# First messages as one tile and then three, an earlier clearing of bins, ten supertiles on the first 128 rows: a change to the opening of a graph kernel

## The chip, the cores and the metric

The kernel runs on one core of a Trainium2 chip. The metric is device time in microseconds (us), taken as the median of several executions. The core has five engines that run side by side and wait for one another through semaphores: TensorE (PE, matrix products; its weight loads are shown as PEld), VectorE (DVE), ScalarE (ACT), GpSimd (POOL) and SyncE (SP, which here only issues DMA transfers). ACT and POOL issue some transfers too.

## The reference

A layer of a graph network over 12,500 nodes with 128 features and 400,000 edges with 20 attributes. The edges are sorted by `dst`.

```
h    = relu(layernorm(x))                       # 12500 x 128
hW   = h @ W_in2f.T
Wij  = smu(edge_attr @ W_f1.T + b_f1) @ W_f2.T + b_f2
Wij  = Wij * edge_weight[:, None]               # 400000 x 128
msg  = hW[dst] * Wij                            # gather: dst is sorted
agg  = segment_sum(msg, src, 12500)             # scatter: src is random
out  = x + smu(agg @ W_o1.T + b_o1) @ W_o2.T + b_o2
smu(x) = ((1+a)x + (1-a) x erf(mu (1-a) x)) / 2,  a = 0.01, mu = 2.5
```

`smu` is computed as a scaled GELU plus a linear part.

## The kernel before

**Tiles.** 128 edges are a tile, 4 tiles a group (`GRP`), 8 tiles a supertile (`SUP`), so two groups make a supertile. There are 3125 tiles. The 12,500 nodes are 98 bins of 128 rows (`NB`). The supertiles are cut into ten epochs (`PARTS`: 59, 59, 59, 59, 48, ...). Each epoch has an area in device memory with room for a fixed number of rows for each bin; three areas (`buf`) are used in turn and are cleared beforehand.

**One group's way.** The helpers below are called by hand, in a written order that is each engine's order (the tile pools run under a manual schedule). For group g:
- `load` (SP) fetches the edge attributes into one of four filter buffers `fbufs` (128 rows by 1024 columns: 20 attribute rows, a row of ones for the bias, and further rows of ones that meet zero weights); `targets` fetches `rbc`, the edges' `dst` less a base, spread over all partitions; `window` fetches rows of h into `hw`.
- `pick` (DVE) or `pick_part` (ACT, two instructions a group) turns `rbc` into a one-hot matrix `oh`. The first `FEW` tiles use no window: their `dst` all lie in the first 128 rows, whose three bfloat16 parts are in `h_first`. Supertile 0 is picked by `pick_group` (DVE) from `dst` values that PE spread with transposes (`spread_group`).
- `hide` (PE, L625, `pu`), `bend` (ACT, L633, GELU, `ge`), `smooth` (DVE, L641, `sm`), `weigh` (PE, L678, `pw`): the filter network.
- `gather` (PE; L657 three products with `h_first`, L659 one with a window; `ph`), `take` (ACT, L667, `hg`), `mix` (DVE, L688, `mt`): the message, features on partitions.
- `turn` (PE, L699, four transposes, `pt`), `send` (ACT, L712 and L715, edge weight, `ms`), `scatter` (POOL, L726): four indirect transfers a group, one for each tile, each of which writes 128 message rows to the places in `ix`.
- `bins` (DVE, L556), `count` (PE, L570 to L573), `read` (DVE, L600), `number` (DVE, L612) find those places: a running count of each bin's rows.

In the main loop, iteration p does `turn`, `send`, a `step`, `number`, `weigh`, `gather`, `take`, `mix` (of the next group), a `step`, `hide`, `bend`, `count`, `smooth` (of the group after it), `pick_part`, `bins`, `read`, and a `step`. From the second epoch on, pieces of work on the epoch before (`parts`, L771 and L787) lie between.

**Steps.** `step` is called three times a group. It first empties the list `opening` (one entry a call): the normalized rows of bins 1 to 3 (`heads`, six stages) and the first 512 tiles' bases and bins (`one`: `based`, `spread`, `lowered`, `turned`, `written`, `bounded`, `binned`). After that it spreads some 280 further steps over the rest of the first epoch: the same for six more chunks of 512 tiles (`head_of`; `spread` is L353, `based` L344 to L348, `binned` L320 to L323, `limits` L377 and L378), the statistics and the h rows of the other bins, which `window` reads. `clear` in `chores` writes zeros to the areas through SP.

**Before the loop.** Loads on SP and ACT, constants on DVE and POOL, then by hand: the first `dst` values (`dsf`), row statistics of bin 0, its normalized, turned and rectified rows, `product` with `w_in`, the three parts `h_first` (`first_part`, `other_parts`), all stages of group 0, and most of group 1. The ACT table for GELU is loaded at L881, behind the square root of the deviations of bins 1 to 3. `quiet_ends` runs on POOL behind five small DVE writes (L425): zeros, the clearing of the last bin (L187, `buf<-zero`), fills of filter buffers 2 and 3. The scatters wait for the landing of that clearing.

## Time and profile before

| what | value |
|---|---|
| median of 3 runs | 4059.88 us (4059.31, 4059.88, 4063.59) |
| profiled execution, its own time | 4063.85 us |
| profiled execution, span of the core | 4062.1 us |
| granted TensorE clock over the span | 0.968 of full speed |
| busy: PE, PEld, DVE, ACT, POOL | 86%, 55%, 82%, 73%, 75% |
| scatters on POOL | 3125, the first at 19.4 us, the last at 3991.2 us |
| bytes moved | 760 MB, 187 GB/s |

A row of a timeline gives the start, the duration, the engine, the line, the operation with its output and inputs, the shape and the number of instructions that were merged; the bracket at its end gives the engine's idle time before it and what ended it. A row by stretches gives the length of the stretch, the busy time and instruction count for each engine, the granted clock, the DMA share and GB/s. Before the first clock record (at 9.6 us) the clock is shown as 1.00.

### The profile page before, as it was taken

Reading aid. Unit: us, or ns where it says so; the run is one execution under the profiler, and the core shown is the slowest. Engines: PE = TensorE matmul, PEld = TensorE weight load, DVE = VectorE, ACT = ScalarE, POOL = GpSimd, SP = SyncE. Lnnn points to the kernel's source line nnn. Section 1 sums busy time; section 2 is a strip of 40 time slices with the busy share of each in tenths; the row PEclk is TensorE's granted clock in tenths of the full one; section 3 lists DMA queues with packets and bytes.
Section 4 is the critical chain, followed back from the end, with each engine's and each line's share of the span. In section 5 each row is a group of like instructions: output and inputs, shape, how many; then the busy total and the mean of one; then the engine's idle time right before and its main releaser. Section 6 shows DMA issues by size and latency. Waiting matters only on the chain.

```text
span 4062.1 us, 69847 instructions
## 1 busy us (share of the span) xinstructions
PE 3492.8 (86%) x18417; PEld 2246.9 (55%) x18420; DVE 3328.4 (82%) x7355; ACT 2962.7 (73%) x7256; POOL 3042.2 (75%) x3168
## 2 busy tenths in 40 slices
PE   7777777999988999989999979999899979989657
PEld 3334434555555555555555546666566646656547
DVE  8987776888887888878888878888799869988447
ACT  5779986888886888877888877787777767766001
POOL 6777777777777777777777777777777777777775
PEclk9999998999999999999999999999999989999889
DMA  6976666777756565546565646666566657565987
GB/s 193 240 187 182 190 167 197 210 204 204 208 162 180 174 175 173 173 141 181 174 177 172 176 144 181 182 180 189 154 193 195 183 156 203 170 202 170 274 240 226
DMA packets 510392, 759.72 MB, mean 187 GB/s; under 512 B 174949, under 2 KB 313462, under 8 KB 509856
## 3 DMA queue, kind: packets, MB, share of 16 engines
q1 hardware_dynamic: 402416, 535.77, 48.4%
q0 software_dynamic: 100112, 207.06, 15.3%
q10 hardware_dynamic: 7456, 12.35, 0.8%
q8 instruction: 146, 2.39, 0.3%
q14 instruction: 262, 2.15, 0.2%
HBM read 460.77 MB, written 294.11 MB: 186 GB/s over the span
## 4 chain that ended last, share of the span: by engine, by line
PE 41%; DVE 26%; DMA 13%; ACT 9%; issue 6%; POOL 4%; ACTq 0%; SPq 0%; DVEq 0%; POOLq 0%
PE pw L678 13%; DMA buf<-ms,ix 10%; PE pg L787 10%; DVE se L771 9%; PE pu L625 7%; PE pt L699 7%; DVE mt L688 5%; POOL buf L726 4%; DVE sl L600 3%; ACT ms L715 3%; ACT ge L633 2%; DVE sm L641 2%; PE ph L659 2%; DVE so L556 2%; DVE agg L800 2%
## 5 line engine op out<-in xcount | busy, mean ns | idle before, releaser
L726 POOL DMA_INDIRECT buf<-ms,ix x2944 | 2829.0, 961 | 916.0 <-issue 270.6
L787 PEld LDWEIGHTS pg<-se,rw 128*128 128x128 f32 x8232 | 1080.8, 194 | 343.3 <-issue 277.1
L787 PE MATMUL pg<-se,rw 128*128 128x128 f32 x8232 | 1175.7, 282 | 96.4 <-DVE se L771 75.1
L715 ACT ACTIVATE ms<-pt,w_sb 128x128 f32<-128x128 f32 x3125 | 882.2, 363 | 196.8 <-PE pt L699 176.0
L556 DVE SCALAR_TENSOR_TENSOR so<-irow_ps,hi_f,so 128x98 f16<-128x98 f32 x2936 | 929.7, 317 | 78.0
L678 PE MATMUL pw<-sm,w_f 128*128 128x512 f32 x1564 | 884.1, 648 | 47.9 <-DVE sm L641 46.9
L625 PE MATMUL pu<-f,w_f 128*128 128x512 f32 x1564 | 813.6, 602 | 0.0
L633 ACT ACTIVATE ge<-pu 128x512 f32<-128x512 f32 x782 | 468.0, 598 | 443.6 <-PE pu L625 439.4
L771 DVE TENSOR_TENSOR se<-irow_ps,rw 128x1536 f32<-128x1536 f32 (+2 forms) x356 | 602.3, 1692 | 229.5 <-DMA rw<-buf 228.3
L699 PE MATMUL pt<-ident,mt 128*128 128x128 f32 x2944 | 468.9, 282 | 362.7 <-DVE mt L688 361.1
L688 DVE SCALAR_TENSOR_TENSOR mt<-pw,b,hg 128x512 f32<-128x512 f32 x782 | 583.4, 746 | 173.3 <-ACT hg L667 149.8
L641 DVE SCALAR_TENSOR_TENSOR sm<-pu,ge 128x512 f32<-128x512 f32 x782 | 534.2, 683 | 188.2 <-ACT ge L633 182.4
L699 PEld LDWEIGHTS pt<-ident,mt 128*128 128x128 f32 x2944 | 327.6, 142 | 447.2 <-DVE mt L688 444.4
L524 ACT ACTIVATE oh<-oh,onesb 128x512 bf16<-128x512 bf16 x770 | 555.5, 721 | 25.2
L523 ACT ACTIVATE oh<-rbc,nrow 128x512 bf16<-128x512 bf16 x770 | 551.2, 716 | 1.2 <-DMA rbc<-rel_dram 1.2
L667 ACT ACTIVATE hg<-ph 128x512 f32<-128x512 f32 x782 | 472.1, 604 | 99.9 <-PE ph L659 30.3
L600 DVE TENSOR_REDUCE sl<-pc 128x4 f32<-128x392 f32 x782 | 434.5, 556 | 0.0
L678 PEld LDWEIGHTS pw<-sm,w_f 128*128 128x128 f32 x1564 | 236.5, 191 | 161.8 <-DVE sm L641 124.7
L659 PE MATMUL ph<-oh,hw 126*128 126x512 bf16 x770 | 298.2, 387 | 0.0
L625 PEld LDWEIGHTS pu<-f,w_f 128*128 128x128 f32 x1564 | 256.9, 196 | 67.2 <-issue 57.9
L570 PE MATMUL pc<-so,tri 128*128 128x392 f16 x736 | 243.7, 331 | 1.7 <-DVE agg L425 1.7
L572 PEld LDWEIGHTS <-rest_h 128*128 128x128 f16 x781 | 76.7, 98 | 263.6 <-issue 263.6
(192 smaller groups left out, 2002.1 us busy)
## 6 DMA issues: line engine op xcount, KB each, us to landing
rw<-buf SPq DMA_DIRECT2D x300, 774.0 KB
rbc<-rel_dram SPq DMA_DIRECT2D x389, 256.0 KB
buf<-zero SPq DMA_DIRECT2D x146, 387.0 KB
buf<-ms,ix POOLq DMA_INDIRECT x2944
rw<-buf SPq DMA_DIRECT2D x49, 645.0 KB
f<-in_f_t SPq DMA_DIRECT2D x390, 80.0 KB
hw<-h_dram SPq DMA_DIRECT2D x770, 31.5 KB
kept_rows<-ms ACTq DMA_DIRECT2D x45, 258.0 KB
```

Of the source, the lines that this page charges most:

```text
L524: nc.scalar.activation(oh, oh, AF.Relu, scale=-1.0, bias=onesb[:, 0:1])
L556: nc.vector.scalar_tensor_tensor(so[:, j], irow_ps[:, :NB], hi_f[:, t + j:t + j + 1], so[:, j - 1] if j else before, op0=ALU.is_equal, op1 ...
L600: nc.vector.tensor_reduce(sl[:, :n], pc[:, :n], op=ALU.max, axis=AX.X)
L625: nc.tensor.matmul(pu[:, :n], w_f1, loaded[g // PER][0][:, o:o + n], start=True, stop=True)
L641: nc.vector.scalar_tensor_tensor(sm[:, :n], units_of.pop(g)[:, :n], LIN, hidden[g][:, :n], op0=ALU.mult, op1=ALU.add)
L678: nc.tensor.matmul(pw[:, :n], w_f2, hidden.pop(g)[:, :n], start=True, stop=True)
L688: nc.vector.scalar_tensor_tensor(mt[:, :n], pws.pop(g)[:, :n], b2, rows_of.pop(g)[:, :n], op0=ALU.add, op1=ALU.mult)
L699: nc.tensor.transpose(pt[:, j, :], mt[:, j * P:(j + 1) * P], ident)
L715: nc.scalar.activation(ms[:, j, 0:P], pt[:, j], AF.Copy, scale=w_sb[:, t + j:t + j + 1])
L726: i = nc.gpsimd.indirect_dma_start(out=bufs[k][:, :], out_offset=bass.IndirectOffsetOnAxis(ap=ix[:, j:j + 1], axis=0), in_=ms[:, j, :], in ...
L771: nc.vector.tensor_tensor(se[:, a:a + n], own.unsqueeze(1).to_broadcast([P, n, P]), rows_in[c][:, a:a + n, P:P + 1].to_broadcast([P, n, P] ...
L787: nc.tensor.matmul(pgs[0][:, g, :], rows_in[c][:, o, 0:P], sel[c][:, o, :], start=(q == 0), stop=(q == Q[k] - 1))
```

## The change

All of it is in the opening, but for the K range of `hide` and the rate of `step`.
- Group 0 is cut into its first tile (128 columns) and the other three (384 columns); the first tile's transposes, send and scatter stand ahead of the rest, and each tile is turned, sent and scattered by itself.
- The zeros and the clearing of the last bin are the first things that POOL does behind the constants; `quiet_ends` and its five DVE touches are gone.
- Constants for counting are made while the first loads are under way; `irow_ps` and the scaling of `w_f2` move to ACT; eight products that nobody reads (`idle`) stand first on PE.
- The deviations of bins 1 to 3 and the GELU table load stand ahead of `product`; their reciprocals become the first entry of `opening`.
- `FEW` is ten supertiles, not six; all but supertile 0 are picked on ACT with `pneg` as bias, and `pick` on DVE is gone.
- Only 21 rows of `w_f1` and of a filter buffer are read by `hide`; one buffer is filled with ones, the ones row is copied to the three others by DMA.
- `opening` takes an entry on every second call, and the later steps are spread over seven groups fewer.

```diff
+    def early_constants():
+        nc.vector.memset(onesb, 1.0)
+        nc.vector.memset(ones_h, 1.0)
+        nc.vector.memset(none, 0.0)
         nc.vector.tensor_scalar(lift, ident, BIG, None, op0=ALU.mult)
         nc.vector.scalar_tensor_tensor(tri, irow, pcol, lift, op0=ALU.is_gt, op1=ALU.add)
-        nc.vector.memset(ones_h, 1.0)
         nc.vector.tensor_sub(rest_h, ones_h, tri)
-        nc.vector.memset(none, 0.0)
+        nc.vector.tensor_scalar(pneg, pcol, -1.0, None, op0=ALU.mult)
+        nc.vector.memset(ones1, 1.0)
+        nc.vector.memset(bad, 0.0)
...
-        FEW = 6 * SUP
+        FEW = 10 * SUP
...
-        nc.sync.dma_start(ds, dst_col[:, 0:FEW])
         nc.scalar.dma_start(x_sb[:, 0:1, :], bin_rows(x, 0, 1))
         nc.sync.dma_start(ss, src_col[:, 0:FEW])
+        nc.scalar.dma_start(x_sb[:, 1:HEAD, :], bin_rows(x, 1, HEAD - 1))
         nc.scalar.dma_start(w_in, w_in_t)
+        nc.sync.dma_start(ds, dst_col[:, 0:FEW])
         fill(0, nc.vector)
-        fill(1, nc.vector)
-        nc.vector.tensor_copy(irow_ps, irow)
-        nc.gpsimd.memset(w_f1, 0.0)
+        early_constants()
+        nc.sync.dma_start(fbufs[0][0:R, :], f_t[:, 0:SUP * P])
         nc.sync.dma_start(w_f1[0:R, :], w_f1_t)
...
         nc.scalar.activation(spare[:, 0:1], eps, AF.Sqrt)
+        nc.scalar.activation(irow_ps, irow, AF.Copy)
+        nc.gpsimd.memset(zero, 0.0)
+        clear(0, len(cleans) - 1, nc.gpsimd)
+        nc.gpsimd.dma_start(h_dram[NB * P:N + P, :], zero[:N + P - NB * P, 0:3 * D // 2].bitcast(BF))
+        nc.gpsimd.memset(x_sb[:, NB - 1, :], 0.0)
+
+        def more_loads():
+
+            for i in range(1, NF):
+                nc.sync.dma_start(fbufs[i][R:R + 1, :], fbufs[0][R:R + 1, :])
+            load(1)
+            one["fetched"]()
+            nc.sync.dma_start(w_sb[:, FEW:CH], w_col[:, FEW:CH])
...
-            if s < FEW // SUP:
-                if i == 0:
-                    pick(s)
-                return
...
-            nc.scalar.activation(oh, loaded[s][1][:, o:o + n], AF.Abs, bias=nrow)
+            nc.scalar.activation(oh, loaded[s][1][:, o:o + n], AF.Abs, bias=pneg if s < FEW // SUP else nrow)
             nc.scalar.activation(oh, oh, AF.Relu, scale=-1.0, bias=onesb[:, 0:1])
...
-            nc.tensor.matmul(pu[:, :n], w_f1, loaded[g // PER][0][:, o:o + n], start=True, stop=True)
+            nc.tensor.matmul(pu[:, :n], w_f1[:R + 1], loaded[g // PER][0][:R + 1, o:o + n], start=True, stop=True)
...
+        def idle(n):
+            for _ in range(n):
+                nc.tensor.matmul(pt[:, 0:P], onesb, onesb, start=True, stop=True)
...
+        def turn_tile(j):
+            nc.tensor.transpose(pt[:, j * P:(j + 1) * P], mt[:, j * P:(j + 1) * P], ident)
+
+        def send_tile(j, ix):
+            nc.scalar.activation(ms[:, j, 0:P], pt[:, j * P:(j + 1) * P], AF.Copy, scale=w_sb[:, j:j + 1])
+            scatter_tile(0, ms, ix, j)
+
+        one_cut, others = (0, P), (P, (GRP - 1) * P)
+        idle(8)
+        stats(edge, 0)
+        nc.scalar.activation(rstd[:, 0:1], mv[:, 0:1, 1], AF.Sqrt, bias=eps)
+        nc.vector.tensor_copy(dsf, ds)
+        nc.vector.tensor_copy(ssf, ss)
+        stats(edge, 1)
+        scaled_means(0, 1)
         normed()
+        nc.tensor.transpose(pw[:FEW, 0:P], dsf, ident)
+        spread_tiles(0, pb0, 0, 2)
         turned()
+        nc.scalar.activation(few, pw[:FEW, 0:P], AF.Copy)
+        nc.sync.dma_start(rel_dram[0, 0:FEW * P].rearrange("(t e) -> t e", e=P), few)
+        more_loads()
+        for b in range(2, HEAD):
+            stats(edge, b)
+        shorn()
+        nc.scalar.activation(rstd[:, 1:HEAD], mv[:, 1:HEAD, 1], AF.Sqrt, bias=eps)
+        nc.scalar.activation(spare[:, 1:2], eps, AF.Gelu)
+        rounded(hi_f[:, 0:FEW], ssf)
+        bins(0)
+        hide_cut(*one_cut)
+        product()
+        spread_tiles(0, pb0, 2, 2)
+        first_part()
+        bend_cut(*one_cut)
         pick_group(0, pb0)
+        nc.scalar.activation(w_f2, w_f2, AF.Copy, scale=GC)
         other_parts()
         count(0)
+        gather_cut(*one_cut)
+        smooth_cut(*one_cut)
+        take_cut(*one_cut)
+        weigh_cut(*one_cut)
+        hide_cut(*others)
         read(0)
         number(0)
+        ix0 = taken.pop(0)
+        few_places()
+        mix_cut(*one_cut)
+        nc.scalar.activation(ms[:, :, P], lo_b[:, 0:GRP], AF.Copy)
+        bend_cut(*others)
+        gather_cut(*others)
+        turn_tile(0)
+        send_tile(0, ix0)
+        smooth_cut(*others)
+        weigh_cut(*others)
+        take_cut(*others)
         targets(1)
         load(2)
         targets(2)
+        pb1 = bank("pb")
+        spread_tiles(1, pb1, 0, GRP)
+        mix_cut(*others)
+        bins(1)
+        for j in range(1, GRP):
+            turn_tile(j)
+            send_tile(j, ix0)
         hide(1)
+        count(1)
         bend(1)
         pick_group(1, pb1)
         smooth(1)
         read(1)
-        pick(1)
+        pick_part(PER)
         bins(2)
+        pick_part(PER + 1)
...
-        opening = [one["based"], heads[0], one["spread"], heads[1], one["lowered"], heads[2], one["turned"], heads[3],
-                   one["written"], heads[4], one["bounded"], heads[5], one["binned"], other_starts]
+        opening = [lambda: scaled_means(1, HEAD), one["based"], heads[0], one["spread"],
+                   heads[1], one["lowered"], heads[2], one["turned"], heads[3], one["written"], heads[4], one["bounded"],
+                   heads[5], one["binned"], other_starts, rows_in_thirds]
+        apart_by = 0
...
             if opening:
-                opening.pop(0)()
+                apart_by += 1
+                if apart_by % 2 == 0:
+                    opening.pop(0)()
                 return
             slot += 1
-            while taken_steps < COUNT and taken_steps * 3 * (eps_of[0][1] * PER - 15) < slot * COUNT:
+            while taken_steps < COUNT and taken_steps * 3 * (eps_of[0][1] * PER - 22) < slot * COUNT:
```

`hide_cut` to `mix_cut` are the helpers of one group with a range of columns; `scatter_tile` is the body of `scatter`'s loop; `rows_in_thirds` makes `prow` and `nrow` as before.

More of the change, by code (lines that the diff above doesn't have):

```diff
@@ L877, in gnn_kernel @@
-        nc.vector.tensor_scalar(w_o1, w_o1, LIN, None, op0=ALU.mult)
-        for b in range(1, HEAD):
-            stats(edge, b)
-        deviations(1, HEAD)
-        nc.scalar.activation(spare[:, 1:2], eps, AF.Gelu)
-        product()
-        counting_constants()
-        bins(0)
-        quiet_ends()
-        load(1)
-        first_part()
-        bend(0)
+        nc.scalar.activation(few, pw[:FEW, 0:P], AF.Copy)
+        nc.sync.dma_start(rel_dram[0, 0:FEW * P].rearrange("(t e) -> t e", e=P), few)
```

116 lines of the change are left out of this document (49 added, 67 removed).

## The prediction

> **What bounds the kernel now.** I read the costliest groups first, then POOL's scatter by stretches, then the timelines of the opening. The page shows one group that nothing overlaps on its engine:
>
> ```profile
> L726 POOL DMA_INDIRECT buf<-ms,ix x2944 | 2829.0, 961 | 916.0 <-issue 270.6
> ```
>
> These scatters and 181 more of the same line (`ix_kept`) are POOL's whole work. By stretches (us, POOL busy and count, clock, DMA share, GB/s):
>
> ```profile
> 0.00:100.00 100.00, 57.62 (x59) 0.92 0.67 194
> ...
> 800.00:900.00 100.00, 75.92 (x80) 1.00 0.71 202
> ...
> 3700.00:3800.00 100.00, 75.93 (x80) 0.88 0.65 190
> ```
>
> 79 to 80 scatters in each full 100 us, whatever PE, DVE and ACT do: POOL is the bound, 1.264 us a scatter (0.96 busy, 0.30 issue). 3124 such steps are 3949 us. The rest of the 4062.1 us span is the first scatter's start (19.4), 71 us behind the last one (3991.2), and 23 us in which POOL waited. So I keep one number, the **zero line**: start of scatter n minus 1.264 n. Only what raises it costs time; the other engines' work is free while messages lie ready ahead of POOL. POOL's timeline, where it rises (second column: duration; bracket: idle before):
>
> ```profile
> 13.03 0.77 POOL L187 DMA_DIRECT2D buf<-zero  x1
> ...
> 19.42 1.05 POOL L726 DMA_INDIRECT buf<-ms,ix  x1 [3.59 <-ACT ge L633]
> ...
> 25.42 0.96 POOL L726 DMA_INDIRECT buf<-ms,ix  x1 [1.10 <-ACT ms L715]
> ...
> 64.21 0.96 POOL L726 DMA_INDIRECT buf<-ms,ix  x1 [3.17 <-ACT ms L715]
> ...
> 81.24 0.96 POOL L726 DMA_INDIRECT buf<-ms,ix  x1 [1.83 <-ACT ms L715]
> ```
>
> They are scatters 0, 4, 32 and 44: zero line 19.42, 25.42-5.06=20.36, 64.21-40.45=23.76, 81.24-55.62=25.62. Single scatters of 1.2 to 1.4 us bring it to 29.5 by 700 us, and 12.9 us come later, 9 of them in four waits between 2450 and 2639 us. Scatter 0 did not wait for its message (first `ms` write ended 17.41): POOL's first semaphore event on this line is at 18.6, when the zeros issued at 13.03 had landed. Groups 8 and 11 are late because of PE:
>
> ```profile
> 52.56 0.66 PE L699 MATMUL pt<-ident,mt 128*128 128x128 f32 x4 [0.28 <-DVE mt L688]
> 56.12 1.12 PE L353 MATMUL pg<-base_f,ones 1*128 1x512 f32 x2 [2.90 <-DVE base_f L345]
> ```
>
> In PE's order L353 (head 1's `spread`) stands behind `turn`, and its input behind `smooth`, `pick`, `bins` and `read` on DVE. The clock then falls, and head 1's `binned` and `limits` (4 us of DVE) follow: turns 7 to 11 start at 52.56 and 79.01, 26.5 us for 20.2 us of POOL. The clock by stretches (PE busy, PEld, DVE, ACT, POOL, clock):
>
> ```profile
> 9.59:13.00 3.41, 1.45 (x8) 0.59 (x7) 2.90 (x17) 1.67 (x6) 1.55 (x2) 1.00 0.00 0
> 13.00:16.41 3.41, 2.49 (x5) 0.92 (x6) 1.84 (x4) 0.45 (x2) 2.83 (x6) 0.50 0.68 184
> 16.41:19.83 3.42, 2.96 (x8) 1.14 (x6) 1.72 (x6) 1.74 (x5) 0.41 (x1) 0.50 0.80 264
> ```
>
> It changes at ends of 3.41 us stretches: down after 1.45 us of matmul, still down after 2.49, up after 2.96.
>
> The durations of the sum are starts to starts in the timelines. A pass of 512 columns on PE: 0.853 cold (L625 at 16.80 and 17.65), 0.427 warm (21.74 and 22.17); fp32 products take two passes, transposes one, and results come 0.2 behind. ACT in a late group, with picks:
>
> ```profile
> 66.05 0.60 ACT L633 ACTIVATE ge<-pu 128x512 f32<-128x512 f32 x1
> 66.53 0.73 ACT L523 ACTIVATE oh<-rbc,nrow 128x512 bf16<-128x512 bf16 x1
> 67.29 0.72 ACT L524 ACTIVATE oh<-oh,onesb 128x512 bf16<-128x512 bf16 x1
> 67.92 0.19 ACT L712 ACTIVATE ms<-lo_b 128x4 f32<-128x4 bf16 x1
> 68.02 1.12 ACT L715 ACTIVATE ms<-pt,w_sb 128x128 f32<-128x128 f32 x4
> ```
>
> `bend` 0.5, two pick instructions 1.4, and only then the sends: a pick on ACT delays its group's messages by 1.4 us, where the DVE pick that it replaces (0.48 for two groups) stood beside them.
>
> **First message.** DVE loses the second fill (0.91) and gains constants (`lift` 0.22, `tri` 0.35, `rest_h` 0.23, memsets about 0.3): `down` ends near 5.0, as before (5.08). Eight `idle` products of two 0.213 passes hold PE from 2.1 to 5.5; behind them three transposes end at 6.1, so `turned` runs as before and xT is ready at 6.9. `product` no longer stands behind a 512-column `hide` (6.40 to 8.39) but behind 128 columns (0.43). The deviations of bins 1 to 3 need DVE's statistics, now done near 6.0, not 8.2; so the table load (1.28) runs 7.2 to 8.5 and `first_part` starts 8.65, not 9.97. DVE then runs the residual 0.28, `pick_group` 0.74, third part 0.29, `smooth` 0.25, `read` 0.56, `number` 0.16, `few_places` 0.21, `mix` 0.27: 11.4. PE is later: 3 x 0.107 gather to 10.2, weigh 0.43 to 10.75, the other 384 columns of `hide` 2 x 0.64 to 12.0 and of `gather` 3 x 0.32 to 13.0, and `turn_tile(0)`, behind them in its order, to 13.4. `send` 0.37 and POOL's 0.28: first scatter 14.1; 14.6 if the first needs the 0.8 us seen between 18.6 and 19.42. The zeros are issued near 2.3 and land, at 5.5 us as before, by 8, under cover of 6 us. Uncovered bound: they share the DMA engines with the first loads and could delay those 1 to 2 us; `w_f2` and `w_sb` have 3 us.
>
> **Second message, second group.** Tile 1 waits for bend 0.48, smooth 0.53, weigh 2 x 0.64, mix 0.57, turn, send: 16.8 cold, 15.8 warm. The turns share one `pt` bank and alternate with sends, 0.85 a tile, so `hide(1)` starts at 17.4 cold or 16.4 warm (before: 16.80) and its `bend` at 19.3 or 17.5 (before: 18.75). Here the moved picks count: behind `bend(1)` ACT has four pick instructions (2.8), `take` 0.5, `bend(2)` 0.5, two picks 1.4, `ms` 0.1, send 0.37, and POOL 0.28: scatter 4 comes 6.5 behind `bend(1)` (before 6.67, on DVE's picks and a half-cold PE). Zero line at scatter 4: 19.0 if warm throughout, 20.9 if cold only until 19.8, 23.2 if cold until `hide(2)`. From 9.59 to 13.0 PE would have 2.98 us of matmul, so it rises at 13.0; the next stretch has about 1.5, next to the 1.45 that fell. I take 20.0. So five us at scatter 0 become 0.4 at scatter 4.
>
> [...]
>
> **Groups 2 to 13.** `heads[0]` puts 1.2 us of normalizing on ACT ahead of `send(2)`: +0.3. Then ACT needs 3.6 us a group with picks (65.08 to 69.24 with a 0.5 extra), PE 3.9; before, with opening steps at full rate, turns 1 to 7 took 4.75 each. At half rate I take 4.35, 0.7 below POOL's 5.06: by group 13 some 8 us lie ahead. Head 1's `based` and `spread` fall on the third and first step of groups 12 and 13, the same bad order, now against 8 us of cover, with 6.3 us of stall. So the rise from 20.72 to 25.62 goes, but for its 0.3 of slow scatters: -4.6. Without the cover it stays. The two extra gather matmuls of 8 groups (0.43 each) lie in PE's spare 1 us. Steps then run 280 in 288 slots, not 309: about 0.1 us more ACT a group in the h rows, where ACT is 97% busy and messages lie 10 us ahead; nothing. 21 rows: L353's one-row pass took 0.59, as L625's 128 rows; nothing. The three copies of the ones row stand in SP's order before `load(1)`, about 1 us, with 8 us until `hide(2)`; nothing.
>
> Edits with one answer, nothing, each under a wait or the cover: `irow_ps` copied on ACT (0.3) while it waits for the statistics; the `w_f2` scaling (0.27) while it waits for the residual; `w_o1`'s scaling (0.22) and the five row-number steps (0.7) later on DVE; POOL's fills and DVE's five touches (0.3) gone; `ss` ahead of `ds` on SP (0.4), both landed before DVE gets to them.
>
> **Sum.** Zero line at 700 us: 20.0 + 0.3 + slow scatters as before (0.36 + 0.34 + 3.9) = 24.9, against 29.5: -4.6. The profiled execution took 4063.85 us, 4 us above the median 4059.88 of 4059.31 to 4063.59; off the median: **4055.3**.
>
> **Rivals.** (a) *A cold opening*, 0.17: scatter 4 at 23.2 and a cover of 4 us: 23.2+0.3+2+4.6=30.1, +0.6: 4060.5. For it: 1.5 us of matmul is next to the 1.45 that fell. Against: four full-rate groups recover 0.7 each. (b) *Warm throughout, and the late waits shift too*, 0.17: -5.6, and part of the 9 us at 2450 to 2639, which hang on leads of a few us: -5.6-4=4050, at most 4046. Against: nothing edited is near. (c) *Slower: the clock's monitor counts rows*, 0.06. L625 is 813.6 of PE's 3492.8 us; at 21 of 128 rows a full cold stretch would count 0.81 of 3.41 us, between 2.49 (0.73, stays cold) and 2.96 (0.87). If below the threshold, each of 33 cold stretches (clock 0.968 over the span) lasts one more, 1.7 us of PE; at nine epoch ends there is no lead: +15: 4075. The zeros in those rows before speak neither way.
>
> **Numbers.** Forecast and its spread (4053 to 4059) 0.60. This measurement tells 0.2%, 8.1 us, from no change; the whole opening holds 29.5-14.5-4.6=10 us. So faster 0.16 (b), same 0.77, slower 0.07 (c and unknown ordering). Range 4047.5 to 4063.
>
> **What would show it.** First scatter at 14 to 14.6, second 15.8 to 16.8, fifth at 24 to 26; 62 to 64 scatters in the first 100 us, not 59; no POOL wait over 1 us behind the fourteenth `turn`; 1.264 unchanged. Wrong: a wait of several us between scatters 8 and 60, or the first behind 17.

## The result, and the profile after

| kernel | median, us | runs | ratio to the kernel before, 95% interval |
|---|---|---|---|
| before | 4059.6 | 4 (4059.27 to 4063.59) | |
| after | 4112.73 | 4 (4104.45 to 4118.5) | 1.0128, 1.0116 to 1.014 |

Slower by 53 us, where 4.6 us less was forecast. The profiled execution of after took 4111.77 us (span 4109.9 us, granted clock 0.952; before 4062.1 us and 0.968).

POOL's scatters in after, by stretches of 100 us. The columns: length, POOL busy and count, clock, DMA share, GB/s.

```profile
0.00:100.00 100.00, 57.43 (x60) 0.86 0.62 179
...
200.00:300.00 100.00, 70.91 (x74) 0.74 0.64 186
...
800.00:900.00 100.00, 75.61 (x80) 1.00 0.71 208
```

The pace of 80 in 100 us is still there at 800 us, with the same 0.96 us a scatter (below, 960 ns). It is missing from 100 to 700 us: 72 to 77 a stretch, where the granted clock is 0.74 to 0.93. From the page of after, the engines' busy time, the clock in 40 slices and two groups:

```profile
PE 3748.2 (91%) x18454; PEld 2240.6 (55%) x18459; DVE 3333.9 (81%) x7345; ACT 2970.8 (72%) x7280; POOL 3037.0 (74%) x3164
...
PEclk8877989999999999999999999999999989999879
...
L725 POOL DMA_INDIRECT buf<-ms,ix x2944 | 2826.8, 960 | 979.4 <-issue 281.4
...
L620 PE MATMUL pu<-f,w_f 21*128 21x512 f32 x1562 | 901.0, 657 | 0.0
```

One engine has more to do than before: PE, 3748.2 us in place of 3492.8, for practically the same number of products. The group at L620 is `hide`, now with 21 rows; the same group had 813.6 us (mean of one 602 ns) on 128 rows.

**The zero line** (start of scatter n less 1.264 n, in us) shows where time is lost. The rows below are one profiled execution each (in the third and fourth row the slowest of its kernel's runs, 9 and 12 us above their median; the others lie within 5 us of theirs); the last column is the change from the kernel before at scatter 3124.

| kernel | 0 | 4 | 60 | 500 | 2100 | 3124 | to before |
|---|---|---|---|---|---|---|---|
| before | 19.4 | 20.4 | 25.7 | 29.5 | 39.9 | 42.4 | |
| after | 12.5 | 23.4 | 25.2 | 62.5 | 86.4 | 91.2 | +48.8 |
| after, `hide` on 128 rows | 16.0 | 21.6 | 22.5 | 29.8 | 44.9 | 47.9 | +5.5 |
| before, `hide` on 21 rows | 19.3 | 24.0 | 38.0 | 67.6 | 99.6 | 105.1 | +62.7 |
| before, `hide` on 64 rows | 19.3 | 21.4 | 28.3 | 35.9 | 59.4 | 64.2 | +21.8 |
| before, `hide` on 96 rows | 19.4 | 20.6 | 28.6 | 33.0 | 42.3 | 44.1 | +1.7 |
| before, extra 21-row product | 19.4 | 19.6 | 27.2 | 36.2 | 126.8 | 137.4 | +95.0 |

In after, at scatter 60 (100 us) nothing is lost: 25.2 against 25.7. From scatter 60 to 500 the line rises by 37.3, against 3.8 before: 33.5 us. From 500 to 2100 it rises by 23.9 against 10.4: 13.5 us. The rest adds 2.4.

Two stretches with all engines tell these two losses apart. The columns: length, PE, PEld, DVE, ACT and POOL busy (count), clock, DMA share, GB/s. Before, and then after:

```profile
100.00:700.00 600.00, 452.31 (x1880) 236.42 (x1880) 472.25 (x1261) 500.84 (x1250) 456.21 (x472) 0.94 0.71 194
700.00:2850.00 2150.00, 1948.91 (x10252) 1243.32 (x10251) 1845.11 (x4052) 1719.71 (x4217) 1623.71 (x1694) 0.99 0.62 179
```

```profile
100.00:700.00 600.00, 508.21 (x1732) 225.31 (x1730) 454.42 (x1222) 478.03 (x1185) 432.73 (x446) 0.84 0.63 184
700.00:2850.00 2150.00, 2046.78 (x10137) 1216.76 (x10136) 1828.69 (x4019) 1699.65 (x4183) 1608.31 (x1680) 0.99 0.59 178
```

In the first stretch 26 scatters are missing (33 us at 1.264), and the clock went from 0.94 to 0.84. In the second 14 are missing (18 us) although the clock is 0.99 in both: there PE is simply busier, 2046.78 against 1948.91 us. So a change of K, which removes work on paper, gave PE more work at full clock, and half the clock for more of the time.

POOL's opening in after (columns as in the timelines of the prediction):

```profile
12.51 1.04 POOL L725 DMA_INDIRECT buf<-ms,ix  x1 [8.63 <-DVE sm L876]
15.89 0.97 POOL L725 DMA_INDIRECT buf<-ms,ix  x1 [2.33 <-ACT ms L895]
...
28.46 0.95 POOL L725 DMA_INDIRECT buf<-ms,ix  x1 [9.08 <-ACT ms L710]
```

The first message leaves 6.9 us earlier than before, and POOL then waits 9.08 us for group 1. PE by stretches there (columns as above; the clock is that of the stretch itself):

```profile
8.80:12.21 3.41, 2.43 (x11) 1.13 (x10) 2.52 (x8) 1.55 (x6) 0.00 (x0) 1.00 0.68 208
12.21:15.63 3.42, 2.92 (x7) 1.57 (x7) 1.50 (x5) 0.76 (x3) 1.04 (x1) 0.50 0.82 279
...
25.87:29.28 3.41, 3.41 (x10) 1.74 (x10) 2.63 (x8) 3.05 (x8) 0.82 (x1) 0.50 0.00 0
```

The clock falls behind a stretch in which PE was busy for 2.43 of 3.41 us. Four stretches with 2.76 to 3.20 us don't bring it back; the fifth, with 3.41 us and no product on 21 rows in it, does (29.28). In the kernel before a stretch with 2.96 was enough.

### The profile page after: what moved, and what is told of

Its sections match the earlier page's. It is cut to its first block, busy times and chain, and to the rows that moved or that the text cites. A ratio compares the mean times of both kernels' runs of the same rounds, so it can differ in the third digit from the quotient of the medians.

```text
span 4109.9 us, 69887 instructions
## 1 busy us (share of the span) xinstructions
PE 3748.2 (91%) x18454; PEld 2240.6 (55%) x18459; DVE 3333.9 (81%) x7345; ACT 2970.8 (72%) x7280; POOL 3037.0 (74%) x3164
## 4 chain that ended last, share of the span: by engine, by line
PE 61%; DVE 20%; ACT 6%; DMA 6%; issue 4%; POOL 4%; ACTq 0%; DVEq 0%; SPq 0%; POOLq 0%
PE pw L673 16%; PE pg L786 14%; PE pu L620 13%; PE pt L694 8%; DVE se L770 7%; DVE mt L683 4%; DMA buf<-ms,ix 3%; POOL buf L725 3%; PE ph L654 3%; PE pc L565 3%; DVE sl L595 2%; DVE sm L636 2%; ACT ge L628 2%; ACT ms L710 1%; PE pc L567 1%
## 5 line engine op out<-in xcount | busy, mean ns | idle before, releaser
L673 PE MATMUL pw<-sm,w_f 128*128 128x512 f32 x1562 | 897.8, 658 | 41.1 <-DVE sm L636 39.2
L620 PE MATMUL pu<-f,w_f 21*128 21x512 f32 x1562 | 901.0, 657 | 0.0
L519 ACT ACTIVATE oh<-oh,onesb 128x512 bf16<-128x512 bf16 x780 | 562.8, 721 | 25.6
L694 PEld LDWEIGHTS pt<-ident,mt 128*128 128x128 f32 x2940 | 338.9, 145 | 246.7 <-DVE mt L683 240.2
L565 PEld LDWEIGHTS <-tri 128*128 128x128 f16 x782 | 74.9, 96 | 612.1 <-issue 595.3
L620 PEld LDWEIGHTS pu<-f,w_f 21*128 21x128 f32 x1562 | 234.9, 188 | 204.3 <-issue 120.2
L565 PE MATMUL pc<-so,tri 128*128 128x392 f16 x736 | 254.4, 346 | 0.8 <-DVE so L551 0.8
```

What stands on the lines that cost most here:

```text
L519: nc.scalar.activation(oh, oh, AF.Relu, scale=-1.0, bias=onesb[:, 0:1])
L620: nc.tensor.matmul(pu[:, :n], w_f1[:R + 1], loaded[g // PER][0][:R + 1, o:o + n], start=True, stop=True)
L673: nc.tensor.matmul(pw[:, :n], w_f2, hidden.pop(g)[:, :n], start=True, stop=True)
L694: nc.tensor.transpose(pt[:, j, :], mt[:, j * P:(j + 1) * P], ident)
```

## Experiments

Two theories were formed from these rows. *Change-over:* a product on few rows next to one on 128 rows costs PE time of its own, at each passage from one to the other. *Clock:* what decides on the clock counts a product by its rows. The rival to both was that the opening's other edits had lost the time.

**1. All of the change but the 21 rows.** `hide` on 128 rows; filter buffers and `w_f1` filled as in the kernel before, by POOL.

```diff
+        nc.gpsimd.memset(w_f1, 0.0)
...
+        for i in range(1, NF):
+            fill(i, nc.gpsimd)
...
-            for i in range(1, NF):
-                nc.sync.dma_start(fbufs[i][R:R + 1, :], fbufs[0][R:R + 1, :])
...
-            nc.tensor.matmul(pu[:, :n], w_f1[:R + 1], loaded[g // PER][0][:R + 1, o:o + n], start=True, stop=True)
+            nc.tensor.matmul(pu[:, :n], w_f1, loaded[g // PER][0][:, o:o + n], start=True, stop=True)
...
-            nc.tensor.matmul(pu[:, o:o + w], w_f1[:R + 1], fbufs[0][:R + 1, o:o + w], start=True, stop=True)
+            nc.tensor.matmul(pu[:, o:o + w], w_f1, fbufs[0][:, o:o + w], start=True, stop=True)
```

> The changed kernel with `hide` on all 128 rows again (w_f1 zeroed, all four filter buffers filled with ones, no copies of the ones row); every other part of the change stays. Theory ROWS (the 21-row products cost the time: PE passes 0.53 instead of 0.43 us, and a clock that stays low): the zero line passes 700 us at about 25, so 4055 to 4058 us, PE's granted clock 0.965 or more, hide's passes 0.43 apart. Theory OPENING (picks on ACT for ten supertiles, the slower opening and the later steps packed into seven groups fewer starve POOL between groups 13 and 110): still 4100 or more, zero line at 700 us near 60, with hide's passes back at 0.43.

Measured: 4056.6 us (11 runs, 4054.7 to 4065.84) beside 4060.78 of the kernel before (21 runs), ratio 0.9988, 0.9979 to 0.9997. The rest of the change gains 4.2 us, and everything lost came with the 21 rows. (Its profiled execution is the slowest of the eleven, so its row in the table ends higher than its median would.) POOL's opening in it:

```profile
16.01 1.05 POOL L726 DMA_INDIRECT buf<-ms,ix  x1 [9.18 <-ACT ms L896]
18.21 0.98 POOL L726 DMA_INDIRECT buf<-ms,ix  x1 [1.15 <-ACT ms L896]
...
26.62 0.96 POOL L726 DMA_INDIRECT buf<-ms,ix  x1 [4.91 <-ACT ms L711]
```

The first message leaves 3.5 us later than in after. Some 2.4 us of this the experiment brings with it: beside POOL's fills, VectorE's conversions of the first `dst` and `src` values take 2.63 and 2.55 us (0.23 and 0.19 in after, where POOL has no such fills), and both end with the fills.

```profile
4.25 2.63 DVE L903 CAST dsf<-ds 128x80 f32<-128x80 int32 x1 [0.34 <-DMA ds<-in_dst_col]
4.07 2.75 POOL L313 MEMSET f<- 128x1024 f32 x3
```

The line is 21.8 at scatter 8 and 22.0 at scatter 44, where the kernel before rises from 20.7 to 25.6. Messages lay 9.0 us ahead of POOL at groups 12 and 13 and 3.6 us at group 14: the cover held.

**2. The 21 rows alone,** in the kernel before.

```diff
-            nc.tensor.matmul(pu[:, :n], w_f1, loaded[g // PER][0][:, o:o + n], start=True, stop=True)
+            nc.tensor.matmul(pu[:, :n], w_f1[:21], loaded[g // PER][0][:21, o:o + n], start=True, stop=True)
```

> The kernel before with one edit: `hide` reads 21 rows of w_f1 and of the filter buffer. ROWS: slower by 40 to 60 us, 4100 to 4120, PE's clock near 0.95, zero line at 700 us near 60. OPENING: within 5 us of 4059.6, as 21 rows then cost PE at most 0.3 us a group, in its spare time.

Measured: 4113.16 us (4107.32 to 4125.56), ratio 1.0124, 1.0108 to 1.0139, clock 0.946. This one line costs what the whole change costs. Time at half clock: 448 us in 49 spells, against 262 in 33 before and 393 in 43 after; 249, 82 and 208 us of it before 650 us.

**3. A probe ahead of the kernel before:** 24 products of 512 columns each (two passes a product) on 128, 21, 128, 64, 128, 96, 128, 32, 128 rows, and then 24 pairs of 21 and 128, back to back on the same engine.

```diff
+        probe = ps1.tile([P, GRP * P], F32, name="pt")
+
+        def block(rows, count):
+            for _ in range(count):
+                nc.tensor.matmul(probe, onesb[:rows], fbufs[1][:rows, 0:GRP * P], start=True, stop=True)
+
+        block(128, 24)
+        for rows in (21, 64, 96, 32):
+            block(rows, 24)
+            block(128, 24)
+        for _ in range(24):
+            block(21, 1)
+            block(128, 1)
```

> The kernel before with a probe ahead of its opening: 24 products of 512 columns (two passes each) on 128 rows, then on 21, 128, 64, 128, 96, 128, 32, 128 rows, then 24 pairs of a 21-row and a 128-row product; PE is busy all the time. If the monitor counts rows: the clock rises in the first block, falls to half in the blocks of 21 and 32 rows within 3.4 to 7 us of their start although PE never idles, and rises again in each block of 128. If it counts busy time: it stays at 1.00 from the first block's end to the last. Pass spacing: 0.427 within a block; if only changes between row counts cost time, the pairs alone show 0.53, else the 21-row block does.

Measured in one execution, by stretches of one clock (length, then PE, PEld, DVE, ACT, POOL busy and the clock). By the products' starts the 21-row block runs from 25.93 to 62.41, 64 rows from 86.14, 96 from 127.64, 32 from 168.94 to 205.07, the pairs from 227.45 to 296.8:

```profile
6.90:30.80 23.90, 23.90 (x57) 10.36 (x56) 0.00 (x0) 0.00 (x0) 0.00 (x0) 1.00 0.04 13
30.80:68.34 37.54, 37.54 (x45) 14.42 (x44) 0.00 (x0) 0.00 (x0) 0.00 (x0) 0.50 0.00 0
68.34:174.15 105.81, 105.81 (x246) 46.10 (x245) 0.00 (x0) 0.00 (x0) 0.00 (x0) 1.00 0.00 0
174.15:208.29 34.14, 34.14 (x41) 13.17 (x40) 0.00 (x0) 0.00 (x0) 0.00 (x0) 0.50 0.00 0
208.29:256.07 47.78, 47.78 (x100) 16.32 (x99) 0.00 (x0) 0.00 (x0) 0.00 (x0) 1.00 0.00 0
256.07:303.86 47.79, 46.41 (x56) 13.42 (x56) 4.41 (x21) 3.37 (x8) 0.00 (x0) 0.50 0.01 2
```

PE is busy without a gap until 296.8, and yet the clock halves 4.9 us into the 21-row block, 5.2 us into the 32-row block, and after 28.6 us of pairs; it comes back 5.9 and 3.2 us after the 128 rows that follow 21 and 32 have begun. Through the blocks of 64 and 96 rows, 20.8 and 20.6 us long, it stays full. So in this probe the clock does not follow whether PE is busy (23.90 of 23.90 us ahead of the first fall, 37.54 of 37.54 at half clock); it goes with how many rows are. Inside every block, of any number of rows, passes at full clock start 0.43 us apart. Where 128 rows meet 21, 32 or 64, two spacings are longer: the last pass ahead of the change takes 0.52 and the first behind it 0.53, so such a change costs 0.2 us between these products. Where they meet 96 it stays 0.43. Both theories' effects exist; which one costs the time was still open.

**4. 96 rows, 64 rows.** As experiment 2, with 96 or 64 in place of 21.

> The kernel before with `hide` on 96 rows (75 of them meet zero weights or ones). ROWS in two halves: if the loss is mostly that weights of a part of the array are not loaded under the products before (passes 0.53 apart, the same for any number of rows under 128), as slow as with 21 rows. If it is mostly that the clock's monitor counts fewer rows, three quarters of the array count nearly fully, cold stretches end as before, and the time is 4060 to 4075. OPENING: 4060.

Measured: 4060.16 us, ratio 0.9998, 0.9989 to 1.0007. No loss; passes 0.43 apart; half clock 311 us, 49 more than before, at no price. 64 rows:

> The kernel before with `hide` on 64 rows: passes should stand 0.53 apart as with 21 rows (the probe showed that between 64 and 128 rows), but the probe's clock stayed full through a block of 64 rows and fell in 21 and 32. If the loss is the change-over (0.3 us of PE a group): as slow as 21 rows, 4100 to 4120. If it is the clock: most of it gone, 4062 to 4080, with about 300 us of half clock in all (262 before, 448 with 21 rows).

The same kernel again, three times; what each expectation adds is what the one before had left open:

> The kernel before with only the hide on 64 rows (filter and counting products unchanged); the other rows of the input are zeros, so the output is the same. Two theories share the loss that 21 rows cost (52 us when only the hide was changed). Change-over theory: the price is the extra 0.1 us at each passage between products of few rows and of 128; the probe showed it at 64 rows as well (spacing 0.53 at the change against 0.43), so 64 rows pay it as 21 do: hide and its neighbours 0.53, 0.53 apart, PE busy some 150 to 250 us more, time 4100 to 4120. Clock theory: the price is that the clock's monitor counts a 21-row product as little or nothing; in the probe 64 rows kept full clock, so they count in part: half-clock time near the 262 to 310 us of 128 and 96 rows, time 4062 to 4080 although each passage still costs its 0.1 us.

> The kernel before with only the hide on 64 rows. Each passage to and from 128 rows costs 0.1 us as at 21 rows (the matrix engine some 150 to 250 us busier), but in the probe 64 rows kept the full clock. Change-over theory: 4100 to 4120. Clock theory: half-clock time near 262 to 310 us and 4062 to 4080.

> The kernel before with only the hide on 64 rows. Each passage to and from 128 rows costs 0.1 us as at 21 rows, but in the probe 64 rows kept the full clock. Change-over theory: 4100 to 4120. Clock theory: half-clock time near 262 to 310 us and 4062 to 4080.

The kernel with 64 rows was run four times. Three times the chip took 5307 to 5319 us for the kernel before itself: POOL's group waits there 2000 us and more where it waited 916, 8 or 9% of the chain that ended last is put down to another core or an unknown queue, and the scatters do not bound; ratios there were 1.015, 1.0176 and 1.0184. On a chip that takes 4061.02 us for the kernel before: 4086.29 us, ratio 1.0065, 1.0049 to 1.0082. By stretches, as above:

```profile
100.00:700.00 600.00, 505.77 (x1838) 226.94 (x1838) 470.36 (x1250) 496.03 (x1239) 452.50 (x469) 0.89 0.65 193
700.00:2850.00 2150.00, 2046.96 (x10156) 1217.80 (x10154) 1832.17 (x4022) 1701.06 (x4185) 1608.07 (x1680) 0.99 0.59 178
```

In the second stretch this is after to the digit: PE 2047 us, 1680 scatters. Half clock is no part of that loss: from 700 to 2850 us it takes 24 us here and 44 in the kernel before. In the first stretch it is near the kernel before: 469 scatters for 472, not 446. Neither theory's range held it (4100 to 4120 and 4062 to 4080). Its half-clock time is 301 us, near the 311 of 96 rows, which lost nothing, but more of it lies before 650 us: 143 us, against 116 with 96 rows and 82 before.

What belongs to which can be told roughly from POOL's delays behind scatter 60, that is, what a start comes later than 1.264 us after the one ahead, where it is over 0.2 us. Sorted by whether the clock was at half at any time in the 8 us ahead:

| kernel | delays at full clock, us | delays behind half clock, us |
|---|---|---|
| before | 13 | 2 |
| before, `hide` on 96 rows | 15 | 3 |
| before, `hide` on 64 rows | 29 | 10 |
| after | 30 | 38 |
| before, extra 21-row product (experiment 5) | 106 | 6 |

So the change-over alone costs 16 to 17 us with 64 rows and in after, and what goes with the half clock is 8 us with 64 rows and some 36 in after. How much of the latter is change-overs that were made at half clock stays open: no run has the half clock of 21 rows without the passages.

**5. Change-overs without a loss for the clock.** The kernel before with a one-column product on 21 rows ahead of each `hide`, in a column that `hide` then overwrites.

```diff
+            nc.tensor.matmul(pu[:, 0:1], w_f1[:21], loaded[g // PER][0][:21, o:o + 1], start=True, stop=True)
             nc.tensor.matmul(pu[:, :n], w_f1, loaded[g // PER][0][:, o:o + n], start=True, stop=True)
```

> The kernel before with one added product of a single column on 21 rows ahead of each `hide` (overwritten by it): two more change-overs a group, and hardly any loss of what the clock's monitor counts. If the change-over is the cost: PE has 0.3 us more a group, 4085 to 4115. If the clock is: at most 4066, half clock near 270 us in all.

> The kernel before with a product of 21 rows and one column put ahead of each hide, into a column that the hide of 128 rows overwrites. The 128-row hide itself stays, and with it what the clock counts; what is added is the change to 21 rows and back in every group, 782 times. Change-over theory: 0.1 us and more for each of two changes, all of it on the matrix engine: 4085 to 4115. Clock theory: the work that the monitor counts is that of the kernel before, half-clock time stays 260 to 310 us, and the added 0.3 us of a group disappears into the matrix engine's idle time: at most 4066.

> The kernel before with a product of 21 rows and one column put ahead of each hide of 128 rows, into a column that the hide overwrites. Where the kernel before took 5317 us and its messages, not its scatters, set the pace, this cost 196 us at the same clock, 0.25 us of each of 782 groups: the passages' own price where nothing hides them. Where the kernel before takes 4060, change-over theory: the matrix engine's idle time is too scattered to hide 0.25 us of a group, 4085 to 4115 with half-clock time at 260 to 310 us. Clock theory: it hides them, at most 4066; the 52 us of the 21 rows then come from the half clock.

> The kernel before with a product of 21 rows and one column put ahead of each hide of 128 rows, into a column that the hide overwrites: two more passages in every group, 0.25 us of each of 782 groups where nothing hides them (196 us at 5317), and the same work for the clock to count. Where the kernel before takes 4060, change-over theory: 4085 to 4115 with half-clock time at 260 to 310 us. Clock theory: the passages hide in the matrix engine's idle time, at most 4066; the 52 us of the 21 rows then come from the half clock. Sorting the delays of the scatters by the clock in the two profiles gives about 33 us of half clock to 15 of passages, so between the two: about 4075.

Measured: on three chips with 5307 to 5319 us for the kernel before, ratios 1.0388, 1.0367 and 1.0366; on the chip with 4061.02 us, 4157.16 us, ratio 1.0236, 1.0219 to 1.0253. None of the ranges held it. The clock was higher than before (0.978, half clock 185 us), and still 96 us were lost, nearly all in one stretch:

```profile
100.00:700.00 600.00, 499.39 (x2073) 260.92 (x2071) 468.84 (x1247) 493.92 (x1234) 450.28 (x469) 0.96 0.65 192
700.00:2850.00 2150.00, 2081.93 (x10705) 1344.00 (x10704) 1775.04 (x3896) 1636.00 (x4057) 1556.24 (x1626) 1.00 0.56 172
```

The expectation of 0.25 us a group was too low: the five spacings around `hide` (0.205, 0.133, 0.175, 0.533, 0.429) sum to 1.475 us, against 0.973 in the kernel before (0.112, 0.432, 0.429), so 0.50, of which the two small passes themselves are some 0.3; the run tests a change-over together with these. PE's need per group of four scatters from 700 to 2850 us follows from the rows: before 1948.91 / 1694 x 4 = 4.60 us, after and 64 rows 4.87, here 5.12, against POOL's 4 x 1.264 = 5.06. At 5.12, more than POOL needs, 67% of the chain that ended last lies on PE, for 41% before. The loss comes in waits and not evenly: from scatter 500 to 2100 there are 28 of over 0.3 us, most of them 72 scatters apart, where after has 14, 64 rows 15 and the kernel before 6. Why they stand there stays open.

**6. A second supertile picked by one DVE instruction** (experiment 1's kernel otherwise), for a version that beats both.

```diff
+            if s == 1:
+                if i == 0:
+                    nc.vector.tensor_scalar(onehot[s], loaded[s][1], pcol, None, op0=ALU.is_equal)
+                return
```

> The changed kernel on 128 rows, with supertile 1 picked by one DVE instruction (0.48 us) instead of four on ACT (2.8 us ahead of `take(1)` and `send(1)`). If the picks are what holds group 1, as the prediction said: scatter 4 comes 1.5 to 2.5 us earlier, its zero line near 19.5, not 21.6, and 4054 to 4055. If PE's half clock holds it: scatter 4 within 0.5 us of 26.6, and 4056.6 again.

> The change without its 21 rows (hide on 128 rows), and with the picks of the second supertile written by one VectorE instruction and not by four ScalarE ones. The change without its 21 rows had the line through its scatters at 16.0 for the first and 21.6 at group 1, and 4056.6 us. If it is ScalarE's picks ahead of group 1's transposes that hold its first message, the line at group 1 comes down to about 19.5, the cover at the first supertile's stall starts 2 us lower, and the time is 4054 to 4055. If group 1 waits for something else (its products, or VectorE), the line stays at 21.6 and the time at 4056.6 within a microsecond.

> The change without its 21 rows (4056.6 where the kernel before took 4060.8), and with the picks of the second supertile written by one VectorE instruction and not by four ScalarE ones. If ScalarE's picks hold group 1's message, the line through the scatters at group 1 comes down from 21.6 to about 19.5 and the time is 4054 to 4055; if not, the line stays and so does the time.

> The change without its 21 rows (4056.6 where the kernel before took 4060.8), and with the picks of the second supertile written by one VectorE instruction and not by four ScalarE ones. On the chips with 5310 us for the kernel before, the line through the scatters at group 1 stood 0.3 to 2.1 us lower with it (21.4 to 22.3 in three runs) than in the two runs with the picks on ScalarE and the opening on every call (22.6 and 23.5). If ScalarE's picks hold group 1's message, the line there comes down from 21.6 to about 19.5 and the time is 4054 to 4055; if they are worth a part only, to 20.5 to 21 and about 4056; if not at all, line and time stay at 21.6 and 4056.6.

Measured: 1.0013, 1.0039 and 1.0042 on the chips with 5307 to 5319 us; then 4057.42 us beside 4059.51, ratio 0.9994, 0.9985 to 1.0003. The line at scatter 4 stood at 22.3, not below experiment 1's 21.6. ACT was now free for 2.59 us ahead of `take` of group 1, and `take` started at 23.96, where it had started at 23.23: it waits for `gather`. The 0.8 us are no effect of the picks: the first clock record, a rise to full, stands at 18.09 here and at 14.99 in experiment 1, and `bend(1)` starts at 20.77 for 19.99. Scatter 4 follows `bend(1)` by 6.62 us here and 6.63 there. So ACT's picks do not hold group 1. Experiment 1's kernel stays the only one of these with an interval below 1.

**7. The opening's steps at the old rate** (experiment 1's kernel, an entry of `opening` on every call, catch-up from 15):

```diff
-                apart_by += 1
-                if apart_by % 2 == 0:
-                    opening.pop(0)()
+                opening.pop(0)()
...
-            while taken_steps < COUNT and taken_steps * 3 * (eps_of[0][1] * PER - 22) < slot * COUNT:
+            while taken_steps < COUNT and taken_steps * 3 * (eps_of[0][1] * PER - 15) < slot * COUNT:
```

> The changed kernel on 128 rows, with `opening` taken on every call and the later steps spread as before (15 groups left out, not 22). The prediction's cover: messages ahead of POOL by group 13 come from the half rate. If that holds: about 3 us lie ahead when head 1's stall comes at group 8, and the zero line rises there by 2 to 4 us; 4058 to 4061, 2 to 4 us over the kernel with the half rate (4056.6). If picks and order alone give the cover: 4056 to 4057.

> The change without its 21 rows, with the opening's steps put in on every call (the kernel before's rate) and the catch-up begun at 15 in place of 22 calls, which is the old pacing. If the halved rate is what gives the messages their lead of 9 us by group 12, then at the old rate the lead is smaller by 2 to 4 us, the line through the scatters rises behind group 13, and the time is 4058 to 4061. If the lead comes from the early first groups alone, the line stays near 22.5 there and the time is 4056 to 4057.

Measured twice, both times where the kernel before takes 5316 to 5319 us: ratios 1.0032 (1.0004 to 1.006) and 1.0022 (0.9992 to 1.0051). POOL doesn't bound there, so this says nothing on the cover. Whether the half rate or the early start gives the 9 us of lead stays open.

## Why the prediction was wrong, and where it was right

**The step that failed** is one sentence: "21 rows: L353's one-row pass took 0.59, as L625's 128 rows; nothing". It compared durations. A pass's duration runs to its modelled end (0.59 us for one of L625); what the next instruction feels is the distance between starts (0.43 there), and the kernel before already showed that this differs. The two groups, from PE's timeline of the kernel before; of two merged passes the row gives the time from the first's start to the second's end:

```profile
23.02 1.12 PE L353 MATMUL pg<-base_f,ones 1*128 1x512 f32 x2
```

```profile
1001.07 1.02 PE L625 MATMUL pu<-f,w_f 128*128 128x512 f32 x2
```

1.12 against 1.02 is one spacing that is 0.1 us longer; the prediction itself showed a row of L353 with 1.12. The row alone could not have told, since `weigh`, on 128 rows, mostly takes 1.12 behind `turn` as well; but of L353 the second spacing is longer too (0.52), of `weigh` it isn't (0.43). `hide` in after, and then on 96 rows:

```profile
1000.04 1.12 PE L620 MATMUL pu<-f,w_f 21*128 21x512 f32 x2
```

```profile
1000.57 1.02 PE L625 MATMUL pu<-f,w_f 96*128 96x512 f32 x2
```

By starts, the product ahead, `hide`'s first pass and its second pass now last 0.205, 0.533 and 0.520, for 0.112, 0.432 and 0.429: 0.285 us more a group, 223 us over 781 groups, of PE's 255 more. PE's spare time in a group was looked up for the first groups alone ("PE's spare 1 us"), since the prediction took "the other engines' work is free while messages lie ready" as a property of the kernel; it holds as long as PE needs less than 5.06 us a group, and 4.60 leaves 0.46 on average. With 0.29 of it gone, 13.5 us come through at full clock.

The weight loads do not show the loss either: the median load took 0.192 us for L625 on 128 rows, 0.182 for L353 on one row (both in the kernel before) and 0.184 for `hide` on 21 rows in after. What was missing is the price of a change: where 128 rows meet 64, 32 or 21, the probe shows 0.1 us more for the last pass ahead of it, and 0.1 for the first one behind it (0.52 and 0.53 for 0.43). Why a change costs this, and whether the loads have a part in it, is not shown by any run.

**The rival that came true** is (c), at 0.06 and +15 us. It was right as far as the probe goes: with PE busy all the time, the clock fell on 21 and 32 rows (after 4.9 and 5.2 us) and stayed full on 64 and 96. What sets the clock, and whether it counts rows, no run shows. The size failed in two places. It took one more cold stretch for each of the 33 spells, 113 us in all, which is near the 131 us more that after spends at half clock (43 spells); but it let them cost something at nine epoch ends alone, and 126 of the 131 us lie before 650 us, where messages have little lead. There after has 23 spells of 9.1 us on average, for 16 of 5.1. And it had no passages in it. After a fall, PE at half clock could fail to come back even when it had no idle time at all (columns as above, after):

```profile
124.85:128.27 3.42, 3.04 (x4) 1.15 (x5) 3.02 (x10) 0.50 (x1) 2.69 (x3) 0.50 0.76 158
128.27:131.68 3.41, 3.41 (x10) 1.54 (x9) 2.37 (x6) 1.97 (x5) 2.61 (x3) 0.50 0.93 263
131.68:135.09 3.41, 3.41 (x5) 0.65 (x3) 3.30 (x9) 1.78 (x7) 2.38 (x4) 0.50 1.05 271
135.09:138.51 3.42, 3.42 (x10) 1.69 (x10) 2.28 (x7) 2.79 (x8) 1.95 (x3) 0.50 1.04 348
138.51:141.92 3.41, 3.41 (x13) 1.22 (x11) 2.86 (x9) 2.56 (x6) 2.64 (x3) 1.00 1.08 328
```

The two stretches from 128.27 to 135.09 are busy throughout and stay at half; 1.4 and 1.5 us of them are `hide`. The third, as busy, has 0.5 us of `hide`, and the clock is full behind it.

A group takes 5.9 us then (`hide` starts at 127.67 and 133.58), more than POOL's 5.06, and so the first stretch loses time there. Of each cold group, 2 us are `hide`. The rival had taken `hide` at its share of all of PE's work, 813.6 of 3492.8 us; at 2.0 of 5.9 us, and with its own weight of 21 / 128, a busy cold stretch counts 0.72 and not 0.81, below the 0.73 that stayed cold.

How much `hide` counts can be read, with less certainty, from all stretches of 3.41 us. I counted PE's share of each stretch from the starts, with `hide` at a weight, and looked for the one threshold above which a cold clock comes back and the one below which a full clock falls. Misfits, rise and fall together, in each kernel of about 1170 stretches:

| kernel | weight that fits | misfits there | at weight 1 |
|---|---|---|---|
| before, 128 rows | 1 | 2 | 2 |
| before, 96 rows | 1 (0.75: 6) | 3 | 3 |
| before, 64 rows | 0.5 | 11 | 28 |
| after, 21 rows | 0.1 to 0.16 | 6 | 41 |
| before, 21 rows | 0.16 | 11 | 53 |

For 21 and 64 rows the weights are near rows / 128 (0.16 and 0.5), with a rise above some 0.7 to 0.8 and a fall below some 0.4; 96 rows fit 1 better than 0.75. This is a fit, not a measurement, and it is loose: for 21 rows in after, weights from 0 to 0.25 leave 5 to 7 misfits. It does not explain the pairs of the probe, which would count 0.47 (in 2.106 us two passes of 0.427 us at 0.16 and two at 1) and yet fell after 28.6 us. What the probe shows by itself is that 21 and 32 rows fall and 64 and 96 stay for some 20 us. Idle time is no part of that: the clock fell behind 23.90 us in which PE was busy for 23.90, and stayed down with 37.54 of 37.54.

**The opening.** The forecast's first scatter, 14 to 14.6, came at 12.5, with the clock full from 5.39 to 12.21, behind the `idle` products, where half clock had been reckoned; the second came in its range (15.89). The fifth, forecast at 24 to 26, came at 28.46: zero line 23.4, the 23.2 of rival (a), "cold until `hide(2)`". `bend(1)` started at 19.11, as forecast for a cold clock (19.3), but scatter 4 followed 9.35 us behind it and not 6.5, since `hide(2)` at half clock (23.77 to 25.8) stands ahead of group 1's `turn` (26.40) in PE's order. "It rises at 13.0" failed: 2.43 us of matmul, 0.8 of it on 21 rows, ended in a fall at 12.21, and the clock was full again at 29.28. With 128 rows (experiment 1) it was the other way round: the passes up to 14.99 stand at half-clock distances (0.640 for 384 columns), and the first record is a rise there. Each kernel has one profiled execution, the ends of the 3.41 us stretches fall 0.6 us apart in these two, and the fills move the opening of experiment 1; that the rows made the opening of after cold is likely and not shown. In experiment 1 `bend(1)` was later (19.99), and the line was 21.6, not 20.0. Scatter 4 came 6.63 behind `bend(1)`, near the 6.5 forecast, but not for the reason forecast: without the picks on ACT (experiment 6) it is 6.62. That agreement is luck.

**What was right.** POOL's 1.264 us a scatter as bound; the cover at groups 12 to 14, which took the rise from 20.7 to 25.6 away; that a first message 5 us earlier is mostly given back by group 1; and, without the 21 rows, the sum: -4.6 forecast, -4.2 measured, which is within 0.2% as called. That it comes so near is in part luck, since the line at scatter 4 was 1.6 higher than forecast, and no profile shows where the 4.2 us were won: the one of experiment 1 is 9 us above its median, with 29.8 at 700 us for the 24.9 forecast. The other edits priced at nothing cost nothing that can be seen in that time. Of the signs named, after shows 60 scatters in the first 100 us (62 to 64 forecast; experiment 1 has 62), and behind the fourteenth `turn` 26 waits of POOL over 1 us, 59 us in all, where the kernel before has 5 with 11 us, four of which the prediction itself left in place. The point named as making it wrong, a wait of several us between scatters 8 and 60, did not come; the 9.08 us stood ahead of scatter 4, and the loss behind scatter 60, where the prediction had forecast none over 1 us.

## What to carry to other kernels

An instruction on fewer rows was not a smaller one on PE here (a pass of `hide` had a mean of 657 ns on 21 rows, 602 on 128, and with the product ahead of it a group took 0.285 us more): put a price on its neighbours, start to start, before saying "nothing". Where an engine off the bound is nearly as busy as the bound (PE 1948.91 of 2150 us here), work out its need per period against the bound's (4.60 of 5.06 us) ahead of any edit that touches it: only what fits into the spare is free. Padding rows with ones against zero weights looked like waste, and with it the kernel before spent 262 us at half clock, without it 448; 96 rows were as good as 128 (4060.16 us), 64 not (4086.29 beside 4061.02).

## What the runs showed of the hardware

- In the probe the granted clock went with the rows in use: at 100% busy, products on 21 and 32 rows fell to half clock after 4.9 and 5.2 us, blocks of 64 and 96 rows kept full clock for their 20.8 and 20.6 us, and pairs of 21 and 128 rows fell after 28.6 us.
- In the probe, at a change between 128 rows and 64, 32 or 21, the last fp32 pass of 512 columns ahead of it and the first behind it each took 0.1 us longer (0.52 and 0.53 for 0.43); between 128 and 96 they did not.
- In after, PE busy for 3.41 of 3.41 us did not bring the clock back with 1.4 and 1.5 us of it on 21 rows, and did with 0.5.
- Beside POOL's fills of three 128x1024 buffers, two conversions of 128x80 numbers on VectorE took 2.63 and 2.55 us, and 0.23 and 0.19 without the fills.
- The same kernel before took 4060 us on some chips and 5307 to 5319 us on others, where POOL waited over 2000 us in the variants that were profiled, for 916 in the kernel before elsewhere; no run here shows why.
